# Four edits around a decomposed-bias attention: position terms in row halves, earlier q and k weights, tables on another queue, weight sums from the tenth turn

## The chip, the cores and the metric

The kernel runs on one core of a Trainium2 chip. The metric is the device time of one execution in microseconds (us). In this document PE is TensorE (the matrix engine), DVE is VectorE, ACT is ScalarE, POOL is GpSimd and SP is SyncE, which here only issues transfers. PEld is the loading of a matmul's stationary operand, which the profile lists beside PE.

## The reference, cut to what matters

Four layers run one after the other on an image of 48 x 48 positions with 768 channels. Only the first layer is touched: a transformer block with 12 heads of 64 channels, whose attention adds two learned position terms to the scores. T = 2304 is the number of positions.

```python
xn = layernorm(x)
q, k, v = split(xn @ qkv_w + qkv_b)                      # 12 heads, 2304 x 64 each
attn  = (q * scale) @ k.T                                # 2304 x 2304 per head
rel_h = einsum('bhwc,hkc->bhwk', q, Rh)                  # one number per query and key row
rel_w = einsum('bhwc,wkc->bhwk', q, Rw)                  # one number per query and key column
attn  = softmax(attn + rel_h[..., :, None] + rel_w[..., None, :])
x = x + (attn @ v) @ proj_w + proj_b
x = x + gelu(layernorm(x) @ w1 + b1) @ w2 + b2
```

Three more layers (spectral filter, scan, spectral filter) follow and are the same in both kernels.

## The kernel before, in words

**Stages.** The first layer runs as: layer norm with q, k, v and the position terms (`qkv_phase`), attention (`attention_bounded`; `attention_any` is a general version behind a run-time branch, which these inputs don't take), output projection (`proj_phase`), then the two-layer perceptron (`mlp_phase`). Products of float32 matrices with weights use a seven-product scheme for 2 x 2 blocks, so weights are first combined into seven sums.

**qkv_phase** walks three superblocks `sb` of 768 tokens. In each it makes v (line 166), then q and k for six head pairs `pr` (line 297). The combined q and k weights are written to memory in superblock 0 and read back by `load_qk` (line 247) in superblocks 1 and 2, into a ring of three weight tiles (`wqk`). The position terms of a superblock are made in 24 steps that lag behind: each step loads a table `relD` (`tables`, line 381, ring of four tiles), multiplies it with q (line 417 for rows, line 403 for columns) and `split`s the result into three bfloat16 parts on ACT and DVE (lines 373 to 376), which go to memory (`rh_d`, `rw_d`, line 392). `advance` issues the tables of up to three steps ahead. The steps of the last superblock run partly after its last q and k product, in front of the attention. `ahead(0)` loads a small one-hot matrix `oneh` and keys and values of the first head pair (`kv`, lines 527 and 528); `ahead(1)` loads the first chunk of queries and its position terms `bt` (lines 505, 506, 534).

**attention_bounded** works on transposed scores: keys on partitions, queries along the free axis. It walks 6 head pairs x 5 query chunks (`qc`, 464 queries, the last 448) x 18 key tiles `kt` of 128 keys. Three key tiles are a turn; there are 180 turns, and turn `i` issues in this order:

- `products` for three key tiles (line 576): for each of the two heads a float32 matmul with 64 contraction rows, head 0 in the upper half of the array's rows and head 1 in the lower half;
- `scores` for three key tiles: for each head one bfloat16 matmul (line 585) with 120 contraction rows (48 column parts and 72 row parts of the position terms, `bt`, against `oneh`) that adds the position terms in PSUM, then the exponential of both heads on ACT (line 587) into a tile `p`, then an addition on DVE (line 595) for the softmax denominators;
- `values` of turn `i - 1` (line 606): for each head a float32 matmul with 64 output columns, the heads in the two column halves of the array. At the end of a chunk `row_sums` (lines 614 and 616) and `finish` (line 622).

The score tiles `s` have three PSUM buffers and `p` has ten SBUF buffers. Beside this, a generator `other` prepares the weights of the projection and the perceptron (`weight_sums`): in every sixth turn it takes one step, with loads on SP (line 776), combinations on POOL (lines 131 to 134) and stores. Its input tiles (`pw0b` is the first) come out of the ring of `p`. The generator has 29 steps; the turns 3, 9, ..., 177 offer 30.

**What sets the order.** A scheduler fixes every engine's order, SP's included, when the program is built; an engine then works strictly in that order. SP's instructions of all loads and stores stand in one queue, and each waits in its place for what it needs.

Of the kernel before, what the change touches and what calls it, by code (L numbers as in the profile page):

```python
# [182 lines left out]
def qkv_phase(tc, ident, x, qkv_w, qkv_b, relT, rel_d, ln_g, ln_b, q_d, k_d, v_d, rw_d, rh_d, wqk_d, wv_d, flag, home, ahead):  # L183
# [18 lines left out]
    with (  # L202
# [42 lines left out]
        def load_qk(sb, pr):  # L245
            wqks[sb, pr] = w_tile(f"wqk_{sb}_{pr}").rearrange("p (n c f) -> p n c f", n=7, c=NC2)
            nc.sync.dma_start(wqks[sb, pr], wqk_d[pr])
# [22 lines left out]
        def q_and_k(sb, have_q, step):  # L270
# [4 lines left out]
            for pr in range(NC):  # L275
                if sb:
                    if (sb, pr) not in wqks:
                        load_qk(sb, pr)
                    w = wqks.pop((sb, pr))
                else:  # L280
                    w = w_tile(f"wqk_{sb}_{pr}").rearrange("p (n c f) -> p n c f", n=7, c=NC2)
                    wb = wp.tile([P, NC2, P], F32, tag="wb", name=f"wb_{pr}", bufs=2)
                    lo, hi = slice(pr * P, (pr + 1) * P), slice(C + pr * P, C + (pr + 1) * P)
                    nc.sync.dma_start(w[:, 0:2].rearrange("p a c f -> p (a c) f"), wv[:, :, lo])
                    nc.sync.dma_start(w[:, 6], wv[:, NC2:, hi])
                    nc.sync.dma_start(wb, wv[:, :NC2, hi])
# [40 lines left out]
                for o, d, m in ((q[:, pr], q_d, qms), (kt, k_d, kms)):  # L327
                    o = o.rearrange("p b t -> p (b t)")
                    nc.scalar.dma_start(d[pr * P : (pr + 1) * P, tok], o)
                    V.tensor_reduce(m[:, pr, sb : sb + 1], o, axis=AX.X, op=ALU.max, apply_absolute_value=True)  # L330
                if pr == 1 and sb + 1 == NSB:
                    ahead(0)
# [33 lines left out]
        with tc.tile_pool(name="qkv_o", bufs=1, side="right") as op:  # L366
            R = 2 * G

            def split(ps, parts, n):
# [6 lines left out]
                V.tensor_tensor(parts[2], r, parts[1], ALU.subtract)  # L376

            def tables(which, g, n):

                d = qp.tile([P, 4, R], F32, tag="relD", name=f"relD_{which}_{g}_{n}", bufs=4)  # L380
                nc.sync.dma_start(d, rel_d[which, g])
                return d
# [96 lines left out]
            V.tensor_reduce(mx, ps[:1, : 2 * NC], axis=AX.X, op=ALU.max)  # L479
            V.tensor_scalar(flag, mx, SAFE, None, ALU.is_lt)  # L480
            for _ in range(4):
                advance()
# [25 lines left out]


def queries(qc):  # L510

    return slice(qc * QB, min(T, (qc + 1) * QB))


def load_onehot(nc, pool, oneh_d, o):

    f = pool.tile([P, 3, P], F32, tag="onehf", name="onehf")
    nc.sync.dma_start(f[:NBR], oneh_d)
    nc.vector.tensor_copy(o[:NBR], f[:NBR])


def attention_loads(nc, q_d, k_d, v_d, rw_d, rh_d):
# [7 lines left out]
    def chunk(qb, c):  # L530
        pr, qc = c
        q = queries(qc)
        n = q.stop - q.start
        nc.sync.dma_start(qb[0][:, :n], q_d[pr * P : (pr + 1) * P, q])
        for s in range(2):
            load_bias(nc, qb[1][:, s, :, :, :n], rw_d, rh_d, 2 * pr + s, q.start, n)

# [3 lines left out]
def attention_bounded(tc, ahead, oT, beside, load_next):  # L541
# [14 lines left out]
    with (  # L556
# [22 lines left out]
        def scores(c, kt):  # L579
# [3 lines left out]
            ps = scs.pop((c, kt))  # L583
            for s in range(2):
                nc.tensor.matmul(ps[:, s, :n], lhsT=oneh[:NBR, b % 3, :], rhs=held(c)[1][:NBR, s, b // 3, j, :n], start=False, stop=True)  # L585
            p = pp.tile([P, 2, QB], F32, tag="p", name=f"p_{pr}_{qc}_{kt}")[:, :, :n]
# [39 lines left out]
        for i in range(len(work) + 1):  # L626
            if i % 6 == 3:
                next(other, None)
            if i == len(work) - 8:
                load_next()  # L630
            if i < len(work):
# [8 lines left out]
                for kt in range(k0, k0 + KB):  # L640
                    products(c, kt)
                for kt in range(k0, k0 + KB):
                    scores(c, kt)
# [11 lines left out]

def attention_any(tc, ident, oneh, q_d, k_d, v_d, rw_d, rh_d, oT, beside, load_next):

# [8 lines left out]
    with (  # L666
# [8 lines left out]
        ones = cp.tile([1, HD], F32, tag="ones", name="an_ones")  # L675
        nc.vector.memset(ones, 1.0)
        ka = cp.tile([HD, T], F32, tag="ka", name="an_ka")
        vt = cp.tile([P, NT, HD + 1], F32, tag="vt", name="an_vt")
# [632 lines left out]
def block_kernel(ctx: ExitStack, tc: tile.TileContext, a: dict):  # L1311
# [19 lines left out]
    atc = at_stack.enter_context(tc.tile_pool(name="at_c", bufs=1, side="left"))  # L1331
    oneh = atc.tile([P, 3, P], BF16, tag="oneh", name="oneh")

# [3 lines left out]
    def load_ahead(stage):  # L1337
        if stage == 0:
            load_onehot(nc, atc, a["oneh"], oneh)
# [7 lines left out]
        ones = pool.tile([P, HD], F32, tag="ones", name="ones")  # L1347
        nc.vector.memset(ones, 1.0)
        ahead.extend((loads, kvs, qbs, ones, oneh))
# [18 lines left out]
    with which.Else():  # L1368
        attention_any(tc, ident, oneh, q_d, k_d, v_d, rw_d, rh_d, oT, beside, load_pw)
    at_stack.close()  # L1370
# [486 lines left out]
```

## Time and profile before

| | us |
|---|---|
| median of three runs | 3815.2 (3811.54 to 3820.01) |
| profiled execution | 3815.61 |
| its span | 3813.4 |
| qkv and position terms | 0 to 512.6 |
| attention | 512.6 to 1671.2 |
| projection | 1671.2 to 1810 |
| perceptron and part of the next layer | 1810 to 2820 |
| spectral filter, scan, spectral filter | 2820 to 3813 |

The stages are read from the first instruction of each in the timeline. Of the attention's 1158.6 us PE is busy 1153.05, at a granted clock of 1.00. A matmul in float32 stands as two records in the profile, one in bfloat16 as one. A row of a timeline gives start, duration, engine, line, operation, output and inputs, shapes, and in brackets the idle time of the engine before it with what ended it; a row of the waits gives total, times and longest.

### The profile page before, as it was taken

Reading aid. Unit: us, or ns where it says so; the run is one execution under the profiler, and the core shown is the slowest. Engines: PE = TensorE matmul, PEld = TensorE weight load, DVE = VectorE, ACT = ScalarE, POOL = GpSimd, SP = SyncE. Lnnn points to the kernel's source line nnn. Section 1 sums busy time; section 2 is a strip of 40 time slices with the busy share of each in tenths; the row PEclk is TensorE's granted clock in tenths of the full one; section 3 lists DMA queues with packets and bytes.
Section 4 is the critical chain, followed back from the end, with each engine's and each line's share of the span. In section 5 each row is a group of like instructions: output and inputs, shape, how many; then the busy total and the mean of one; then the engine's idle time right before and its main releaser. Section 6 shows DMA issues by size and latency. Waiting matters only on the chain.

```text
span 3813.4 us, 51839 instructions
## 1 busy us (share of the span) xinstructions
PE 3707.4 (97%) x20914; PEld 2168.0 (57%) x20914; DVE 2032.0 (53%) x3070; ACT 1135.3 (30%) x1803; POOL 653.5 (17%) x498
## 2 busy tenths in 40 slices
PE   7999979999999999998999999999999998999998
PEld 4666543333333333345555555555568876996685
DVE  6655455656566666565424433232325567995455
ACT  1323244444444444420310120011013356222342
POOL 3101001111111111025000000000013301981131
PEclk9999989999999999999999999999999999999999
DMA  7655563333332322124334534443454402112345
GB/s 261 209 191 190 182 189 121 114 108 114 102 101 90 101 90 76 50 86 156 133 105 134 172 109 126 134 133 108 125 161 110 112 29 94 40 33 73 98 117 154
DMA packets 276271, 460.28 MB, mean 121 GB/s; under 512 B 50909, under 2 KB 228821, under 8 KB 269527
## 3 DMA queue, kind: packets, MB, share of 16 engines
q1 hardware_dynamic: 266215, 435.94, 37.5%
q10 hardware_dynamic: 9808, 20.94, 1.5%
q8 instruction: 167, 2.74, 0.3%
q14 instruction: 81, 0.66, 0.1%
HBM read 318.49 MB, written 138.31 MB: 120 GB/s over the span
## 4 chain that ended last, share of the span: by engine, by line
PE 87%; DVE 4%; POOL 3%; DMA 3%; ACT 1%; issue 1%; SPq 0%; ACTq 0%; POOLq 0%; DVEq 0%
PE p L886 13%; PE p L949 13%; PE s L576 12%; PE av L606 11%; PE qk L297 6%; PE s L585 6%; PE c L1113 4%; PE v L166 3%; POOL t L1214 2%; PE pj L166 2%; PE f_z L1516 2%; PE f_z L1517 2%; PE f_x L1481 2%; PE so L1291 2%; PE f_u L1531 2%; PE rh L417 1%
## 5 line engine op out<-in xcount | busy, mean ns | idle before, releaser
L595 DVE TENSOR_TENSOR acc<-acc,p 128x928 f32<-128x928 f32 (+1 forms) x480 | 561.6, 1170 | 359.4 <-ACT p L587 328.1
L587 ACT ACTIVATE p<-s 128x928 f32<-128x928 f32 (+1 forms) x540 | 467.9, 940 | 681.5 <-PE s L585 575.1
L949 PE MATMUL p<-w,h 128*128 128x384 f32 x1512 | 492.7, 486 | 0.0
L576 PE MATMUL s<-qt,kv 64*128 64x464 f32 (+1 forms) x2160 | 467.8, 565 | 7.6 <-ACT p L587 5.4
L606 PE MATMUL av<-p,kv 128*64 128x464 f32 (+1 forms) x2160 | 456.3, 557 | 0.0
L949 PEld LDWEIGHTS p<-w,h 128*128 128x128 f32 x1512 | 286.2, 190 | 196.9
L576 PEld LDWEIGHTS s<-qt,kv 64*128 64x128 f32 x2160 | 194.2, 187 | 277.5 <-issue 161.9
L886 PE MATMUL p<-x2nT,w 128*128 128x384 f32 x864 | 293.9, 490 | 3.3 <-issue 3.3
L606 PEld LDWEIGHTS av<-p,kv 128*64 128x64 f32 x2160 | 141.9, 136 | 247.1 <-issue 237.8
L297 PE MATMUL qk<-xnT,wqk 128*128 128x384 f32 x756 | 252.5, 491 | 5.0 <-DMA wqk<-wqk_d 5.0
L1206 PE MATMUL c<-H,bands 128*48 128x96 f32 x5632 | 243.8, 247 | 11.4 <-issue 10.9
L1206 PEld LDWEIGHTS c<-H,bands 128*48 128x48 f32 x5632 | 234.8, 123 | 20.6 <-issue 11.3
L585 PE MATMUL s<-bt,oneh 120*128 120x464 bf16 (+1 forms) x1080 | 241.3, 359 | 0.0
L886 PEld LDWEIGHTS p<-x2nT,w 128*128 128x128 f32 x864 | 165.4, 192 | 119.2 <-issue 6.1
L886 PE MATMUL p<-xT,w 128*128 128x384 f32 x648 | 220.8, 486 | 0.0
L297 PEld LDWEIGHTS qk<-xnT,wqk 128*128 128x128 f32 x756 | 144.6, 193 | 99.8 <-issue 8.3
L585 PEld LDWEIGHTS <-oneh 120*128 120x128 bf16 x1080 | 90.9, 98 | 190.8 <-issue 110.3
L925 POOL TENSOR_TENSOR rr<-rr,ml_b 128x1152 f32<-128x1152 f32 x12 | 31.5, 2622 | 955.6 <-DMA rr<-xr_d 863.6
L881 ACT ACTIVATE h<-h,ml_b 128x384 f32<-128x384 f32 x144 | 88.3, 614 | 346.6 <-DVE h L901 174.3
L1214 POOL TENSOR_TENSOR t<-s,c 128x768 f32<-128x768 f32 x80 | 144.5, 1832 | 179.5 <-DMA bands<-in_bands_dram 168.9
L886 PEld LDWEIGHTS p<-xT,w 128*128 128x128 f32 x648 | 123.1, 190 | 85.9
L616 DVE RECIPROCAL rec<-rs 128x464 f32<-128x464 f32 (+1 forms) x30 | 91.1, 3038 | 98.7 <-PE rs L614 98.7
(322 smaller groups left out, 4792.6 us busy)
## 6 DMA issues: line engine op xcount, KB each, us to landing
w<-w1s_d SPq DMA_DIRECT2D x36, 768.0 KB
w<-w2s_d SPq DMA_DIRECT2D x36, 768.0 KB
w<-w1s_d SPq DMA_DIRECT2D x36, 576.0 KB
w<-in_mlp_w_dram SPq DMA_DIRECT2D x27, 768.0 KB
wqk<-wqk_d SPq DMA_DIRECT2D x12, 1344.0 KB
yu<-f_ys SPq DMA_DIRECT2D x24, 672.0 KB
f_yt<-yu SPq DMA_DIRECT2D x20, 720.0 KB
yu<-f_us SPq DMA_DIRECT2D x18, 720.0 KB
```

The lines of the kernel that those rows point to most:

```text
L166: nc.tensor.matmul(p[:, :TB], lhsT=rhs[n][:, c, t * P : (t + 1) * P], rhs=w[:, c, :], start=c == 0, stop=c == NC2 - 1)
L297: nc.tensor.matmul(p[:, :TB], lhsT=w[:, n, c, :], rhs=ops[sb][n][:, c, :], start=c == 0, stop=c == NC2 - 1)
L576: nc.tensor.matmul(ps[:, s, :n], lhsT=keys[pr % 2][rows, kt * P : (kt + 1) * P], rhs=held(c)[0][rows, :n], start=True, stop=False)
L585: nc.tensor.matmul(ps[:, s, :n], lhsT=oneh[:NBR, b % 3, :], rhs=held(c)[1][:NBR, s, b // 3, j, :n], start=False, stop=True)
L587: nc.scalar.activation(p, ps[:, :, :n], AF.Exp)
L595: nc.vector.tensor_tensor(probs[c], probs[c], p, ALU.add)
L606: nc.tensor.matmul(avs[c][rows, : size(c)], lhsT=vals[pr % 2][:, kt, rows], rhs=p[:, s, :], start=kt == 0, stop=kt == NT - 1)
L886: nc.tensor.matmul(p[:, :TB], lhsT=w[n][:, c, :], rhs=rhs[n][:, c, :], start=c == 0, stop=c == NC2 - 1)
L949: nc.tensor.matmul(ps[t][:, :TB], lhsT=hs[left, f][:, t * P : (t + 1) * P], rhs=wt[:, f % KW2, :], start=f == 0, stop=f == NF2 - 1)
L1113: nc.tensor.matmul(ps[:K, i, :n], lhsT=v[:, c, tok : tok + K], rhs=w[:, cc, c0 : c0 + n], start=cc == NC - 1, stop=cc == 0)
L1206: nc.tensor.matmul(ps[r0 : r0 + G, k // 4, cols], lhsT=bands[:, n - GC, i, :] if gr else bands0[:, n, i, :], rhs=H[:, n, :, d : d + NPR], ...
L1214: GP.tensor_tensor(t, sc[:, ch], c1[:, m0 : m0 + GC].unsqueeze(2).to_broadcast([P, GC, RR, NPR]), ALU.mult)
```

## The change

- **Position terms in row halves.** The 120 contraction rows of a head's position terms are cut into 64 (48 column parts and 16 row parts) and 56 (the other row parts). Head 0 has its rows in partitions 0 to 63, head 1 in 64 to 127, so that all of these matmuls have the same row halves as `products`. Each head and key tile now has two bfloat16 matmuls in place of one. The order within a turn becomes products and scores of the first key tile, then of the second, then of the third. `bt` and `oneh` have new layouts, with new loads (`load_bias_halves`: ten transfers for a stretch of tokens in place of eight; `load_onehot_halves`: four and four copies in place of one and one).
- **q and k weights** are requested two pairs ahead in superblocks 1 and 2, and `ahead(0)` is called after pair 4 of the last superblock in place of pair 1.
- **Last tables on another queue.** After the bound for the branch is computed, `tables` issues on ACT's queue in place of SP's.
- **Weight sums from the tenth turn.** Turn 3 is skipped: the 29 steps use the turns 9 to 177.
- `ones` is set at the start of the program, in another pool. `attention_any` loads its own `oneh`.

```diff
@@ q_and_k
-                    if (sb, pr) not in wqks:
-                        load_qk(sb, pr)
+                    if pr + 2 < NC:
+                        load_qk(sb, pr + 2)
...
-                if pr == 1 and sb + 1 == NSB:
+                if pr == 4 and sb + 1 == NSB:
                     ahead(0)
@@ qkv_phase
+            queue = [nc.sync]
+
             def tables(which, g, n):
                 d = qp.tile([P, 4, R], F32, tag="relD", name=f"relD_{which}_{g}_{n}", bufs=4)
-                nc.sync.dma_start(d, rel_d[which, g])
+                queue[0].dma_start(d, rel_d[which, g])
...
             V.tensor_scalar(flag, mx, SAFE, None, ALU.is_lt)
+            queue[0] = nc.scalar
             for _ in range(4):
                 advance()
@@ new functions
+def load_bias_halves(nc, bt, rw_d, rh_d, c, t0, n):
+    nw = 3 * KTW
+    at = t0
+    while at < t0 + n:
+        sb, t = divmod(at, 2 * TB)
+        m = min(2 * TB - t, t0 + n - at)
+        cols = slice(2 * c * TB + t, 2 * c * TB + t + m)
+        dst = bt[:, :, at - t0 : at - t0 + m]
+        for s in range(2):
+            w = rw_d[s].rearrange("(j k) n b f -> j (k n) b f", j=KJ)[:, :, sb, cols].rearrange("j r t -> r j t")
+            r = rh_d[s].rearrange("(a k) n b f -> a (k n) b f", a=2)[:, :, sb, cols]
+            p0 = s * HD
+            for a in range(2):
+                nc.sync.dma_start(dst[p0 : p0 + nw, a * KJ : (a + 1) * KJ], w)
+                nc.sync.dma_start(dst[p0 + nw : p0 + HD, a * KJ : (a + 1) * KJ], r[a, : HD - nw].unsqueeze(1).to_broadcast([HD - nw, KJ, m]))
+            nc.sync.dma_start(dst[p0 : p0 + NBR - HD, 2 * KJ :], r[:, HD - nw :].rearrange("a r t -> r a t"))
+        at += m
...
+def load_onehot_halves(nc, pool, oneh_d, o):
+    f = pool.tile([P, 2, 3, P], F32, tag="onehf", name="onehf")
+    for s in range(2):
+        p0 = s * HD
+        nc.sync.dma_start(f[p0 : p0 + HD, 0], oneh_d[:HD])
+        nc.sync.dma_start(f[p0 : p0 + NBR - HD, 1], oneh_d[HD:])
+        nc.vector.tensor_copy(o[p0 : p0 + HD, 0], f[p0 : p0 + HD, 0])
+        nc.vector.tensor_copy(o[p0 : p0 + NBR - HD, 1], f[p0 : p0 + NBR - HD, 1])
@@ attention_bounded: scores
-            for s in range(2):
-                nc.tensor.matmul(ps[:, s, :n], lhsT=oneh[:NBR, b % 3, :], rhs=held(c)[1][:NBR, s, b // 3, j, :n], start=False, stop=True)
+            for k in range(2):
+                for s in range(2):
+                    rows = slice(s * HD, s * HD + (NBR - HD if k else HD))
+                    rhs = held(c)[1][rows, 2 * KJ + b // 3 if k else b // 3 * KJ + j, :n]
+                    nc.tensor.matmul(ps[:, s, :n], lhsT=oneh[rows, k, b % 3, :], rhs=rhs, start=False, stop=k == 1)
@@ attention_bounded: the turns
-            if i % 6 == 3:
+            if i % 6 == 3 and i > 3:
                 next(other, None)
...
                 for kt in range(k0, k0 + KB):
                     products(c, kt)
-                for kt in range(k0, k0 + KB):
                     scores(c, kt)
@@ block_kernel
-    oneh = atc.tile([P, 3, P], BF16, tag="oneh", name="oneh")
+    oneh = atc.tile([P, 2, 3, P], BF16, tag="oneh", name="oneh")
+    ones = atc.tile([P, HD], F32, tag="ones", name="ones")
+    nc.vector.memset(ones, 1.0)
...
-        qbs = [(pool.tile([P, QB], F32, tag=f"qt{i}", name=f"qt{i}"), pool.tile([P, 2, 2, KJ, QB], BF16, tag=f"bt{i}", name=f"bt{i}")) for i in range(2)]
+        qbs = [(pool.tile([P, QB], F32, tag=f"qt{i}", name=f"qt{i}"), pool.tile([P, 2 * KJ + 2, QB], BF16, tag=f"bt{i}", name=f"bt{i}")) for i in range(2)]
```

More of the change, by code (lines that the diff above doesn't have):

```diff
@@ L534, in chunk @@
         nc.sync.dma_start(qb[0][:, :n], q_d[pr * P : (pr + 1) * P, q])
-        for s in range(2):
-            load_bias(nc, qb[1][:, s, :, :, :n], rw_d, rh_d, 2 * pr + s, q.start, n)
+        load_bias_halves(nc, qb[1][:, :, :n], rw_d, rh_d, pr, q.start, n)
     return keys_values, chunk
@@ L583, in scores @@
             ps = scs.pop((c, kt))
-            for s in range(2):
-                nc.tensor.matmul(ps[:, s, :n], lhsT=oneh[:NBR, b % 3, :], rhs=held(c)[1][:NBR, s, b // 3, j, :n], start=False, stop=True)
+            for k in range(2):
[3 more added lines that the diff above has]
+                    nc.tensor.matmul(ps[:, s, :n], lhsT=oneh[rows, k, b % 3, :], rhs=rhs, start=False, stop=k == 1)
             p = pp.tile([P, 2, QB], F32, tag="p", name=f"p_{pr}_{qc}_{kt}")[:, :, :n]
@@ L653, in attention_bounded, with attention_any @@
             pass
-def attention_any(tc, ident, oneh, q_d, k_d, v_d, rw_d, rh_d, oT, beside, load_next):
+def attention_any(tc, ident, oneh_d, q_d, k_d, v_d, rw_d, rh_d, oT, beside, load_next):
     nc = tc.nc
@@ L676, in attention_any @@
         nc.vector.memset(ones, 1.0)
+        oneh = cp.tile([P, 3, P], BF16, tag="oneh", name="an_oneh")
+        load_onehot(nc, cp, oneh_d, oneh)
         ka = cp.tile([HD, T], F32, tag="ka", name="an_ka")
@@ L1338, in load_ahead @@
         if stage == 0:
-            load_onehot(nc, atc, a["oneh"], oneh)
+            load_onehot_halves(nc, atc, a["oneh"], oneh)
             kv_tile()
@@ L1344, in load_ahead @@
         pool = at_stack.enter_context(tc.tile_pool(name="at_a", bufs=1, side="left"))
-        qbs = [(pool.tile([P, QB], F32, tag=f"qt{i}", name=f"qt{i}"), pool.tile([P, 2, 2, KJ, QB], BF16, tag=f"bt{i}", name=f"bt{i}")) for i in range(2)]
+        qbs = [(pool.tile([P, QB], F32, tag=f"qt{i}", name=f"qt{i}"), pool.tile([P, 2 * KJ + 2, QB], BF16, tag=f"bt{i}", name=f"bt{i}")) for i in range(2)]
         loads[1](qbs[0], (0, 0))
-        ones = pool.tile([P, HD], F32, tag="ones", name="ones")
-        nc.vector.memset(ones, 1.0)
         ahead.extend((loads, kvs, qbs, ones, oneh))
@@ L1368, in block_kernel @@
     with which.Else():
-        attention_any(tc, ident, oneh, q_d, k_d, v_d, rw_d, rh_d, oT, beside, load_pw)
+        attention_any(tc, ident, a["oneh"], q_d, k_d, v_d, rw_d, rh_d, oT, beside, load_pw)
     at_stack.close()
```

## The prediction

> **What bounds the kernel now.** I read the page first, then the attention's stage, then one turn of it, then the places where PE stands still. PE carries the page, and the attention's three matmuls (lines 576, 585, 606) are a third of its work:
>
> ```profile
> PE 3707.4 (97%) x20914; PEld 2168.0 (57%) x20914; DVE 2032.0 (53%) x3070; ACT 1135.3 (30%) x1803; POOL 653.5 (17%) x498
> ...
> L576 PE MATMUL s<-qt,kv 64*128 64x464 f32 (+1 forms) x2160 | 467.8, 565 | 7.6 <-ACT p L587 5.4
> L606 PE MATMUL av<-p,kv 128*64 128x464 f32 (+1 forms) x2160 | 456.3, 557 | 0.0
> ...
> L585 PE MATMUL s<-bt,oneh 120*128 120x464 bf16 (+1 forms) x1080 | 241.3, 359 | 0.0
> ```
>
> Line 576 idles 7.6 us in 2160 matmuls, the other two never: from 512.6 to 1671.2 only PE's own pace counts. What that pace is made of shows in one turn's weight loads (start, duration), since a pass starts with its load:
>
> ```profile
> 1022.93 0.30 PEld L576 LDWEIGHTS s<-qt,kv 64*128 64x128 f32 x4 [0.73 <-issue]
> 1023.43 0.19 PEld L576 LDWEIGHTS s<-qt,kv 64*128 64x128 f32 x2 [0.20 <-issue]
> ...
> 1024.60 0.19 PEld L576 LDWEIGHTS s<-qt,kv 64*128 64x128 f32 x2 [0.20 <-issue]
> 1025.47 0.90 PEld L585 LDWEIGHTS <-oneh 120*128 120x128 bf16 x6 [0.68 <-issue]
> 1026.75 0.20 PEld L606 LDWEIGHTS av<-p,kv 128*64 128x64 f32 x4 [0.38 <-DVE acc L595]
> 1027.19 0.14 PEld L606 LDWEIGHTS av<-p,kv 128*64 128x64 f32 x2 [0.24 <-issue]
> ...
> 1028.36 0.14 PEld L606 LDWEIGHTS av<-p,kv 128*64 128x64 f32 x2 [0.25 <-issue]
> 1029.23 0.30 PEld L576 LDWEIGHTS s<-qt,kv 64*128 64x128 f32 x4 [0.73 <-ACT p L587]
> ```
>
> A turn lasts 1029.23 - 1022.93 = 6.30. Both heads' passes run together and follow each other at 0.389 in float32 (1023.43 to 1024.60 are three); the bfloat16 ones, one head after the other, at 0.196 (single records). Six of 576, six of 606 and six of 585 make 5.84. The other 0.45 lies at the three changes of shape. Into 576: the last pass of 606 starts at 1028.75 and ends its 0.389 at 1029.14, 0.10 before the next; then the first pass takes 0.50 in place of 0.39, since its load isn't hidden: 0.20 together. Into 585: 1024.60 + 2 x 0.389 = 1025.38, 0.095 early, and 0.01 for the load: 0.105. Into 606: 0.09 and 0.05, 0.14.
>
> PE's other idle time near the change is at the attention's start:
>
> ```profile
> ACT p L587 <- POOL pw0p L133: 9.6, 1, 9.6
> PE rw L403 <- DMA relD_w<-in_relD_dram: 9.3, 4, 5.8
> ```
>
> ```profile
> 504.94 5.48 PE L403 MATMUL rw<-q,relD_w 128*96 128x96 f32 x40 [5.78 <-DMA relD_w<-in_relD_dram]
> 512.66 2.61 PE L576 MATMUL s<-qt,kv 64*128 64x464 f32 x12 [2.24 <-DVE rest_w L374]
> ...
> 518.29 2.72 PE L576 MATMUL s<-qt,kv 64*128 64x464 f32 x12 [1.74 <-ACT p L587]
> ```
>
> ```profile
> 550.67 0.99 POOL L131 TENSOR_TENSOR pw0p<-pw0b,pw0p 128x384 f32<-128x384 f32 x1 [168.65 <-DMA bt<-rw_d]
> ...
> 552.64 2.62 ACT L587 ACTIVATE p<-s 128x928 f32<-128x928 f32 x3 [9.57 <-POOL pw0p L133]
> ...
> 553.64 4.11 PE L576 MATMUL s<-qt,kv 64*128 64x464 f32 x12 [3.65 <-ACT p L587]
> ```
>
> Tables keep PE waiting 9.3 us in four pieces before 512.66. The exponential of the sixth turn waits until POOL gives back `pw0b`, a tile of the ring of `p`; its load was issued at 544.88, behind a saturated queue.
>
> **The change part by part.** In the built order of both kernels PE's sequence outside the attention is the same, so the sum is made in these places.
>
> Row halves. Matmuls of 585 double, but the two heads run side by side, so a key tile still costs two passes of 0.196: 64 rows of both heads, then 56 of both. That they run together is read from 576: two heads' records start 7 ns apart there and share a pass of 0.389. A turn then needs six passes of each as before. What goes is the change into full rows: 576 and 585 have one shape now. 180 turns x 0.105 = 18.9 us. The change into 606 stays. Loads: each bfloat16 load is 0.098 in the records, under a pass of 0.196; the float32 load behind a bfloat16 pass keeps PE 0.105 when it isn't hidden, and 0.105 fits in 0.196.
>
> Here a rule speaks against the change. The row: in line 576 loads of the same row halves start with each pass, and the passes stay 0.389 apart, so nothing of the load shows. The Trainium skill, page "TensorE: Matmul & The Clock Gate", "What overlaps and what doesn't" in its Part 3, says that weight loads overlap matmuls in flight only in another row group. By that rule each of the 1080 bfloat16 double passes would show its load: 0.01 (585's first) to 0.105 (576's first) each, 11 to 113 us. By the row it is 0, which I take, as it is the same rows and the same neighbours.
>
> New order of a turn. The first exponential may start after 1.3 us of a turn in place of 2.9. In the steady state it waits for nothing, gain 0. In the first turn ACT loads its table (1.28 us) behind the first score, so the second turn's 1.74 falls: first score done at 1.45, table to 2.9, exponential to 3.9, PE's first turn 3.5: 0.4 left, gain 1.4. At a chunk's end DVE gets an addition ahead of the reciprocal (3.06): denominators at 4.7 into the turn, then 3.06 + 1.17 + 0.63 gives 9.6, while the next 606 starts at 10.7. Covered by 1.1; without cover 30 chunk ends would cost it.
>
> Weight sums from turn 9. The stall of 3.65 goes, and with it the stretched line 576 behind it (4.11 for 2.54): 5.2 us. What is late next: `pw0b`'s load stands behind the `bt` load that waits for turn 8, like `pw1b` before, which POOL had finished at about 579 with its use at about 590. For the double tiles of the last twelve steps the exponential that waits moves earlier in its chunk (key tile 14 in place of 15). Loads at 1186.5 gave a first store at 1192.1 and a second at 1195.1, landing (estimate, 2.5 more) by 1195 and 1198; the exponentials come 12.6 and 16.5 after the load. Covered by at least 3.
>
> Last tables on ACT's queue. SP drops 14 loads, so that none stands behind the `bt` loads and the `rh_d` store (that is the 5.78). But ACT now casts and issues: 32 casts at some 0.45 in sequence and eight tables at 0.35 (its own stores are 0.33) are 17 us. It may begin when the first column product is done (about 489.4; in the new order ACT takes two of those casts before the row casts), so the last cast comes at 507 to 509 in place of 512.95, and PE's start follows at about 509 instead of 512.66. Gain 3.5; bounds: 9.3, all waits gone, and -3, if the tables land as late as now (4.8 us from issue for two of them) and hold up the casts.
>
> q and k weights, and `ahead`. The wait is 5.0 us for pair 1 at 397.26. SP around it:
>
> ```profile
> 372.50 0.59 SPq L528 DMA_DIRECT2D kv<-v_d  x1
> 373.18 3.04 SPq L392 DMA_DIRECT2D rw_d<-rw  x2
> 376.61 3.71 SPq L236 DMA_DIRECT2D v_d<-v_o  x1
> 380.37 3.73 SPq L247 DMA_DIRECT2D wqk<-wqk_d  x1
> ```
>
> In the new build's order these four stand unchanged; the values of `kv` are still first, although their call moved. Only pairs 2 and 3 pass the keys' load, where nothing waited. Gain 0; up to 5.0 if the queue drains faster. Superblock 1 keeps its order.
>
> Rest. `oneh`: three more loads and three copies of some 0.4 in superblock 0, where PE has no idle time: 0, without cover 1.2. `bt`: ten transfers for eight, 0.4 each on SP, which is free for most of a chunk of 38 us; its partition rows fall from 720 to 496 per head: 0.
>
> Sum: 18.9 + 1.4 + 5.2 + 3.5 = 29.0. The profiled execution took 3815.6, the median of runs 3815.2: 3786.2.
>
> **The rivals.**
>
> Slower: PE drains when the data type changes, not only at a change of tiling. Into 585 both change, so the row can't tell. The new turn has three changes to bfloat16 (0.105 each) and two back (0.20, with an exposed load): 5.84 + 0.20 + 0.315 + 0.40 + 0.14 = 6.90, 0.60 more than now, 108 us less 10 from the start: 3913. It decides from 0.16 us per turn, 32 ns per change of type. Against it: 606 to 576 has one type and loses the same 0.10, so shape alone explains it; and the skill's "TensorEngine Tiling (Array Packing)", Key Properties, names only the tiling mode. By it 18.9 gained, by the rival 108 lost.
>
> The drain stays: passes in halves cost a few ns more each (9 ns on twelve would do), and only the start gains: 3815.2 - 10.1 = 3805.
>
> The start gives nothing: ACT as the table's issuer is as late as SP, and the tile of `p` stalls once elsewhere. 3815.2 - 18.9 - 1.4 = 3795.
>
> **How the numbers follow.** Forecast 0.60 (own range 3778 to 3793), drain stays 0.15, start gives nothing 0.09, drain per type 0.12, more than forecast (pair 1's wait goes too, tables in full: 3775) 0.04. The range 3773 to 3807 leaves out the slow case. About 0.2% (7.6 us) is what a measurement of this kernel can tell from no change. The forecast, 3795 and 3775 and half of the 3805 case are faster: 0.81; the other half of it is nearly all of same, 0.07; slower 0.12.
>
> **What would show it.** A turn of 6.19 with weight loads of 576 and 585 in turn and no gap of 0.1 between them; a turn near 6.9 or passes of 585 further apart than 0.2 prove me wrong. Line 576's idle near 0.4 besides the first start, no exponential waiting for POOL; the attention's first matmul near 509; the 5.0 at line 297 still there.

## The result and the profile after

| | before | after |
|---|---|---|
| median | 3816.15 (3811.54 to 3820.01) | 3788.78 (3788.09 to 3789.85) |
| profiled execution, its span | 3815.61, 3813.4 | 3788.09, 3786.2 |
| attention's first matmul | 512.66 | 511.15 |
| projection's first matmul | 1672.02 | 1646.44 |

The times are in microseconds. The ratio of the medians is 0.9928, with a 95% interval of 0.9913 to 0.9943. By the profiles the changed kernel leads by 1.5 us when the attention begins, by 25.6 when it ends (at the projection's first matmul) and by 27.4 at the last matmul. So the attention itself gave 24.1.

The page after, the lines that answer to those shown of before (line 576 is now 610, 585 is 622, 606 is 643):

```profile
PE 3689.9 (97%) x21994; PEld 2185.2 (58%) x21994; DVE 2049.4 (54%) x3073; ACT 1174.9 (31%) x1803; POOL 668.4 (18%) x498
...
L610 PE MATMUL s<-qt,kv 64*128 64x464 f32 (+1 forms) x2160 | 527.5, 564 | 2.3 <-DVE rest_w L374 2.3
...
L643 PE MATMUL av<-p,kv 128*64 128x464 f32 (+1 forms) x2160 | 455.6, 557 | 0.0
...
L622 PE MATMUL s<-bt,oneh 64*128 64x464 bf16 (+3 forms) x2160 | 301.4, 355 | 0.0
```

The count of position matmuls doubled. Line 610's idle time is 2.3 us, all of it ahead of the first matmul of the attention; the 5.4 that it spent on exponentials is gone. Busy time by line misleads here: 610 went from 467.8 to 527.5 and 622 from 241.3 to 301.4, although a turn got shorter. The ends of matmuls overlap their successors, and where two lines take turns each is charged with its own tail. The timeline of PE gives the turn (start, duration):

```profile
1020.57 1.05 PE L610 MATMUL s<-qt,kv 64*128 64x464 f32 x4
1021.46 0.56 PE L622 MATMUL s<-bt,oneh 64*128 64x464 bf16 x4
1021.85 0.95 PE L610 MATMUL s<-qt,kv 64*128 64x464 f32 x4
1022.63 0.56 PE L622 MATMUL s<-bt,oneh 64*128 64x464 bf16 x4
1023.03 0.94 PE L610 MATMUL s<-qt,kv 64*128 64x464 f32 x4
1023.81 0.56 PE L622 MATMUL s<-bt,oneh 64*128 64x464 bf16 x4
1024.29 2.56 PE L643 MATMUL av<-p,kv 128*64 128x464 f32 x12
1026.78 1.05 PE L610 MATMUL s<-qt,kv 64*128 64x464 f32 x4
```

Two of PEld's rows in the same turn:

```profile
1021.65 0.39 PEld L610 LDWEIGHTS s<-qt,kv 64*128 64x128 f32 x4
1022.25 0.10 PEld L622 LDWEIGHTS <-oneh 64*128 64x128 bf16 x2 [0.20 <-issue]
```

A turn is 1026.78 - 1020.57 = 6.21, where it was 6.30. Read the distances of starts: two float32 passes 1021.85 to 1022.63 are 0.78, which is 2 x 0.389; two bfloat16 passes 1021.46 to 1021.85 are 0.39, which is 2 x 0.196. Neither change of type leaves a gap: the weights of the product at 1021.85 are loaded from 1021.65 on, in the same rows, while the last bfloat16 pass runs. Over all turns of 464 queries the median went from 6.303 to 6.207, of 448 queries from 6.103 to 6.007.

The waits of PE from 300 to 560 us and the start of the attention:

```profile
PE rw L405 <- DMA relD_w<-in_relD_dram: 5.6, 5, 4.3
PE qk L297 <- DMA wqk<-wqk_d: 4.7, 1, 4.7
PE bound L479 <- DVE pz L475: 3.3, 1, 3.3
PE s L610 <- DVE rest_w L374: 2.3, 1, 2.3
```

```profile
502.76 1.56 PE L405 MATMUL rw<-q,relD_w 128*96 128x96 f32 x8 [4.26 <-DMA relD_w<-in_relD_dram]
...
511.15 1.05 PE L610 MATMUL s<-qt,kv 64*128 64x464 f32 x4 [2.32 <-DVE rest_w L374]
512.00 0.82 PE L622 MATMUL s<-bt,oneh 64*128 64x464 bf16 x4
512.55 1.82 PE L610 MATMUL s<-qt,kv 64*128 64x464 f32 x4
...
522.56 1.05 PE L610 MATMUL s<-qt,kv 64*128 64x464 f32 x4
```

PE still waits for the tables, 5.6 us in place of 9.3. The first turns run slow: a group of four matmuls of line 610 takes 1.82, and 0.95 later. The first two turns take 522.56 - 511.15 = 11.41, where before they took 524.71 - 512.66 = 12.05.

### The profile page after: what moved, and what is told of

Same layout as the page of the kernel before. It is cut to its first block, busy times and chain, and to the rows that moved or that the text cites. A ratio compares the mean times of both kernels' runs of the same rounds, so it can differ in the third digit from the quotient of the medians.

```text
span 3786.2 us, 54130 instructions
## 1 busy us (share of the span) xinstructions
PE 3689.9 (97%) x21994; PEld 2185.2 (58%) x21994; DVE 2049.4 (54%) x3073; ACT 1174.9 (31%) x1803; POOL 668.4 (18%) x498
## 2 busy tenths in 40 slices
DMA packets 259478, 448.23 MB, mean 118 GB/s; under 512 B 47426, under 2 KB 212018, under 8 KB 252724
## 5 line engine op out<-in xcount | busy, mean ns | idle before, releaser
L632 DVE TENSOR_TENSOR acc<-acc,p 128x928 f32<-128x928 f32 (+1 forms) x480 | 574.2, 1196 | 308.9 <-ACT p L624 274.1
L624 ACT ACTIVATE p<-s 128x928 f32<-128x928 f32 (+1 forms) x540 | 507.1, 939 | 620.0 <-PE s L622 616.4
L610 PE MATMUL s<-qt,kv 64*128 64x464 f32 (+1 forms) x2160 | 527.5, 564 | 2.3 <-DVE rest_w L374 2.3
L622 PE MATMUL s<-bt,oneh 64*128 64x464 bf16 (+3 forms) x2160 | 301.4, 355 | 0.0
L622 PEld LDWEIGHTS <-oneh 64*128 64x128 bf16 (+1 forms) x2160 | 108.4, 93 | 259.9 <-issue 255.7
L1244 PE MATMUL c<-H,bands 128*48 128x96 f32 x5632 | 244.2, 247 | 12.2 <-issue 10.9
L1244 PEld LDWEIGHTS c<-H,bands 128*48 128x48 f32 x5632 | 234.5, 123 | 22.1 <-issue 11.3
L1554 PE MATMUL f_z<-f_w,f_o 97*96 97x96 f32 x800 | 133.6, 249 | 0.0
```

What stands on the lines that cost most here:

```text
L610: nc.tensor.matmul(ps[:, s, :n], lhsT=keys[pr % 2][rows, kt * P : (kt + 1) * P], rhs=held(c)[0][rows, :n], start=True, stop=False)
L622: nc.tensor.matmul(ps[:, s, :n], lhsT=oneh[rows, k, b % 3, :], rhs=rhs, start=False, stop=k == 1)
L624: nc.scalar.activation(p, ps[:, :, :n], AF.Exp)
L632: nc.vector.tensor_tensor(probs[c], probs[c], p, ALU.add)
L1244: nc.tensor.matmul(ps[r0 : r0 + G, k // 4, cols], lhsT=bands[:, n - GC, i, :] if gr else bands0[:, n, i, :], rhs=H[:, n, :, d : d + NPR], ...
L1554: nc.tensor.matmul(out, lhsT=o1[:, j, 1:3, :].rearrange("c r h -> c (r h)"), rhs=w2t[:, b, 0, :], start=True, stop=False)
```

## The experiments

Each ratio is against the kernel before on the same chip, whose median there lies between 3817.0 and 3820.03. The first row and those with "alone" are edits of the kernel before, the others of the changed kernel.

| kernel | median | ratio, interval |
|---|---|---|
| full rows, alternating order | 3921.13 | 1.0270 (1.0256 to 1.0284) |
| row halves, grouped order | 3796.93 | 0.9946 (0.9932 to 0.9960) |
| weight sums from the tenth turn alone | 3812.9 | 0.9988 (0.9981 to 0.9994) |
| last tables on ACT's queue alone | 3816.03 | 0.9999 (0.9991 to 1.0008) |
| row halves and alternating order alone | 3796.97 | 0.9950 (0.9936 to 0.9963) |
| q and k two pairs ahead alone | 3819.56 | 1.0003 (0.9995 to 1.0011) |
| changed, tables on SP's queue again | 3790.78 | 0.9926 (0.9912 to 0.9939) |
| changed, SP's queue, five tables ahead | 3786.52 | 0.9919 (0.9906 to 0.9933) |
| changed, pair 1's weights on ACT's queue | 3780.35 | 0.9904 (0.9889 to 0.9919) |
| the last two together | 3775.34 | 0.9890 (0.9873 to 0.9906) |
| that, with the tables on ACT's queue | 3779.77 | 0.9898 (0.9881 to 0.9914) |

### Is it the shape or the data type, the halves or the order?

Two kernels, each with one of the two parts of the edit (row halves, new order). The kernel before with products and position terms in turn, full rows:

```diff
                 for kt in range(k0, k0 + KB):
                     products(c, kt)
-                for kt in range(k0, k0 + KB):
                     scores(c, kt)
```

> The kernel before with one edit: products and scores of a key tile follow each other, with the position terms still in 120 full rows. A turn then has six changes of tiling in place of three. Theory A (each change of shape drains PE for 0.10 us and shows the next load: 0.105 into the position terms, 0.20 back into the products): a turn is 6.303 + 2 x 0.105 + 2 x 0.20 = 6.91 us, the kernel about 110 us slower than before, near 3925. Theory D (the 0.10 belongs to the end of a long group of matmuls and not to the change of shape): the turn stays near 6.3 and the time near 3815.

Its PE timeline, one turn:

```profile
1026.24 1.05 PE L576 MATMUL s<-qt,kv 64*128 64x464 f32 x4
1027.22 0.56 PE L585 MATMUL s<-bt,oneh 120*128 120x464 bf16 x2
1027.72 1.05 PE L576 MATMUL s<-qt,kv 64*128 64x464 f32 x4
...
1033.16 1.05 PE L576 MATMUL s<-qt,kv 64*128 64x464 f32 x4
```

The turn is 6.92. A key tile takes 1027.72 - 1026.24 = 1.48, where the halves take 1.18 (1023.03 - 1021.85). The price of a change of shape, read before from a single place, holds at three: 5.84 + 3 x (0.20 + 0.105) + 0.14 = 6.90. Four position matmuls in halves cost PE the same 0.39 as two in full rows, so nothing but the changes differs.

The changed kernel in grouped order, so that the type changes once each way in a turn where it changed three times:

```diff
                 for kt in range(k0, k0 + KB):
                     products(c, kt)
+                for kt in range(k0, k0 + KB):
                     scores(c, kt)
```

> The changed kernel with the old order inside a turn: the products of three key tiles, then the scores of three. Theory A (the gain is the row halves: products and scores have one shape, the order does not matter): a turn stays at 6.20 to 6.21 us in place of 6.303 before and 6.207 after, and the time stays within 3 us of the changed kernel; only the second turn waits longer for the first exponential again (about 1 us). Theory B (the alternation is what saves): a turn goes back to about 6.30, 17 us slower than the changed kernel. Theory C (a change of data type costs something small, and alternating pays it five times more per turn): a turn is shorter than 6.207, down to 6.19.

```profile
1022.81 2.61 PE L610 MATMUL s<-qt,kv 64*128 64x464 f32 x12
1025.25 1.35 PE L622 MATMUL s<-bt,oneh 64*128 64x464 bf16 x12
1026.53 2.56 PE L643 MATMUL av<-p,kv 128*64 128x464 f32 x12
1029.02 2.61 PE L610 MATMUL s<-qt,kv 64*128 64x464 f32 x12
```

The turn is 6.21 again (median 6.209 against 6.207). Two more changes of type each way cost nothing that shows; the drain is that of the shape. The order is worth something at the two ends: in this profile the first two turns take 13.41 instead of 11.41, and from the last turn's first product to the projection 10.85 pass instead of 9.74, so that the lead at the attention's end is 3.5 us smaller than the changed kernel's. The time missed the 3 us of the expectation: the lead over the kernel before is 20.1 us by the medians, 7.3 less than the changed kernel's. In the profiles the other 3.6 us arise behind the attention, where the code is the same, and stay unexplained.

### The weight sums

```diff
-            if i % 6 == 3:
+            if i % 6 == 3 and i > 3:
                 next(other, None)
```

> The kernel before with the weight sums from turn 9 alone. Theory A: the exponential of the sixth turn no longer waits for POOL; 5.2 us less (ratio 0.9986), all of it in turns 5 and 6 (10.02 and 8.59 us become 6.30 and 7.08), every other turn as before. Rival: the tile pw0b is late one chunk later, and the same wait shows in turn 11 or 12; then 0 to 2 us less.

PE's timeline around the place of the stall, where line 576 stood at 553.64 behind 3.65 of idle time:

```profile
551.38 2.61 PE L576 MATMUL s<-qt,kv 64*128 64x464 f32 x12
...
558.46 2.61 PE L576 MATMUL s<-qt,kv 64*128 64x464 f32 x12
```

There is no idle time here, and the turn at a chunk's end takes 558.46 - 551.38 = 7.08, as later ones do. Its attention began 1.5 us later than before's and its first row sums came 3.8 earlier: 5.2 us gained. By the medians 4.1 us of it are seen (the kernel before had 3817.0 on this chip).

The row halves and the new order with the three other edits undone show what the stall does beside them. The edits, made to the changed kernel:

```diff
-                    if pr + 2 < NC:
-                        load_qk(sb, pr + 2)
+                    if (sb, pr) not in wqks:
+                        load_qk(sb, pr)
...
-                if pr == 4 and sb + 1 == NSB:
+                if pr == 1 and sb + 1 == NSB:
...
-            queue[0] = nc.scalar
...
-            if i % 6 == 3 and i > 3:
+            if i % 6 == 3:
```

> The changed kernel with three of its edits undone: weight sums again from the fourth turn, the last tables again on SP's queue, q and k weights and ahead(0) as before. What is left is the row halves and the alternating order. Theory A (the turn's 0.096 us is the drain at the change of shape, and edits add up): 180 turns x 0.096 = 17.3 us, about 0.5 us in the first two turns, about 1.1 us at the attention's end, no gain before the attention: turns of 6.21, the stall of about 5 us near the sixth turn is back, attention start within 1 us of 512.7, and the total about 18 to 19 us under the kernel before, ratio 0.9951. Rival (the edits lean on each other; part of the 17.3 or of the end's 1.1 needs the stall removed): total within 15 us of the kernel before, ratio 0.996 or more.

PE's timeline, then ACT's, then POOL's (the products stand in line 609 here):

```profile
539.85 1.05 PE L609 MATMUL s<-qt,kv 64*128 64x464 f32 x4
...
554.42 1.92 PE L609 MATMUL s<-qt,kv 64*128 64x464 f32 x4 [8.29 <-ACT p L623]
```

```profile
553.42 2.62 ACT L623 ACTIVATE p<-s 128x928 f32<-128x928 f32 x3 [15.01 <-POOL pw0p L133]
```

```profile
551.45 0.99 POOL L131 TENSOR_TENSOR pw0p<-pw0b,pw0p 128x384 f32<-128x384 f32 x1 [168.94 <-DMA bt<-rw_d]
```

The stall is now 8.29, and the two turns take 14.57 and 9.90 where 6.21 and 6.99 are usual: 11.3 us lost, in place of 5.2. The sum says why. PE reaches this place at 554.42 - 8.29 = 546.13, where before it came at 549.99, 3.86 earlier; POOL's combinations begin at 551.45 in place of 550.67, 0.78 later. The two make 4.64, and the idle time grew by 8.29 - 3.65 = 4.64. The load of `pw0b` was issued at 544.88 before and at 545.15 here, so PE's lead brought it no earlier: what PE gained ahead of the load is given back there to the last tenth. Skipping turn 3 is worth 5.2 us alone and 11 beside the row halves. The rest of the 11.3 is the clock, which is lowered behind the stall (a window; span, busy time and instructions of PE, PEld, DVE, ACT and POOL, then the granted clock, the DMA engines' busy share and GB/s):

```profile
550.15:560.30 10.15, 5.88 (x20) 2.59 (x22) 3.98 (x3) 4.39 (x5) 4.86 (x4) 0.50 0.28 100
```

PE works at half its clock from 554.42 to 560.3 and loses half of these 5.9 us: 8.29 + 2.95 = 11.2. In the kernel before the clock was 0.50 from 553.3 to 556.7, so 3.65 + 1.5 = 5.2.

At the projection the lead is 15.7 us, which the parts make up: 1.6 at the attention's start, where none was expected, 17.3 for the shape, 1.7 in the first two turns, 1.1 at the end, less 6.0 for the longer stall. The total is 20.6 us under the kernel before, near Theory A's 18 to 19, but with the start and the stall mis-sized, and with 3.3 us of lead that appeared behind the attention.

### The last tables

```diff
+            queue = [nc.sync]
+
             def tables(which, g, n):
...
-                nc.sync.dma_start(d, rel_d[which, g])
+                queue[0].dma_start(d, rel_d[which, g])
...
+            queue[0] = nc.scalar
             for _ in range(4):
                 advance()
```

> The kernel before with the last tables on ACT's queue alone. My sum said 3.5 us; the changed kernel's trace shows its attention starting 1.5 us earlier, with three tables held 4.3 us behind a store of row terms and loads of position terms. Theory A (the transfers' common bandwidth, not the issuing queue, sets when these tables land): 1 to 2 us less, PE waits for tables 5 to 7 us before the attention in place of 9.3. Rival (in the old layout the position terms are more bytes in the same stretch, so the tables land later still): 0 to 1 us less.

PE's waits from 300 to 560 in this kernel:

```profile
PE rw L405 <- DMA relD_w<-in_relD_dram: 5.4, 5, 1.9
```

The wait for tables fell from 9.3 to 5.4 and the attention started at 512.72, where it was 512.66. The bound's matmul had come 0.9 later, so that the stretch from it to the attention is 0.9 shorter; of the 3.9 that the wait lost, other links of the chain took 3.0. The first two turns were slower (13.61), the stall of the weight sums was shorter in this profile, and so nothing of it is left in the time. By the medians the kernel is 1.0 us under the one before, inside the noise (0.9991 to 1.0008). The opposite test is the changed kernel without this edit:

```diff
-            queue[0] = nc.scalar
```

> The changed kernel with one edit undone: the last tables again on SP's queue. Theory A (the ACT queue brings nothing, and its four scattered waits let the granted clock fall just as the attention begins): the tables' wait is again one of about 5.4 us plus smaller ones, the attention's first matmul comes within 1 us of 511.15, but at the full clock, so that the first two turns take about 10.2 us in place of 11.41; total within 2 us of the changed kernel, rather below it. Rival (the 1.5 us by which the changed kernel's attention starts earlier came from the queue): first matmul at 512.7 or later, first two turns about 11.4, total 1 to 3 us above the changed kernel.

Its PE timeline:

```profile
505.03 6.07 PE L405 MATMUL rw<-q,relD_w 128*96 128x96 f32 x40 [5.01 <-DMA relD_w<-in_relD_dram]
512.79 1.05 PE L609 MATMUL s<-qt,kv 64*128 64x464 f32 x4 [1.69 <-DVE rest_w L374]
```

Its start, 512.79, is the rival's number and outside the 1 us that I gave; its first two turns, 10.17, are Theory A's. Its median is 2.0 above the changed kernel's, measured on another chip, and the two ratios agree (0.9926 and 0.9928), so the time doesn't tell the two apart. The start has to be counted from the bound's matmul, since this profile reached that one 2.5 us later than the changed kernel's for another reason (6.2 us at line 297). From the bound's second record to the attention's first matmul the profiles give (tables read five ahead left out):

| position terms | tables on SP | tables on ACT |
|---|---|---|
| full rows | 29.82, 29.87, 29.92, 30.01 | 29.01 |
| row halves | 27.83, 27.86 | 28.61, 28.65, 28.67 |

So the queue alone brings 0.9, and loses 0.8 once the position terms are in halves. The halves bring 2.0 with the tables on SP: the last five tables, issued from 499.40 on before and from 501.83 on here, let PE go on 5.5 and 3.2 us later. `bt` in halves has fewer bytes (the whole kernel moves 448.23 MB in place of 460.28), and stands just ahead of these tables on the queue; that the bytes are the reason was not tested by itself.

The clock in the same stretch, first of the changed kernel, then of the one with SP's queue (columns as above):

```profile
510.00:515.00 5.00, 3.85 (x18) 2.29 (x20) 1.92 (x4) 2.98 (x4) 0.00 (x0) 0.72 0.41 84
```

```profile
510.00:515.00 5.00, 3.31 (x25) 2.21 (x26) 3.31 (x7) 2.80 (x7) 0.00 (x0) 0.97 0.01 3
```

With the tables on ACT the attention begins at a clock of 0.72, and its first two turns cost 1.24 more. All five profiles with ACT's queue begin so; of the eight on SP's queue two are slow in these turns as well. What decides can be read from the clock's course. In these traces it is 1.00 or 0.50 and changes on a grid of 3.41 us. The changed kernel's last two steps of this grid around the attention's start, then the step that holds the start in the kernel with SP's queue:

```profile
508.80:512.20 3.40, 1.08 (x8) 0.59 (x9) 3.01 (x6) 1.91 (x4) 0.00 (x0) 1.00 0.00 0
512.20:515.60 3.40, 3.40 (x14) 1.97 (x12) 0.00 (x0) 2.65 (x3) 0.00 (x0) 0.50 0.77 159
```

```profile
510.40:513.70 3.30, 1.61 (x15) 1.05 (x15) 2.83 (x6) 2.19 (x5) 0.00 (x0) 1.00 0.00 0
```

PE is busy for 0.32 of the first and for 0.49 of the last, and only the first is followed by half the clock. In all five profiles with ACT's queue the step ahead of the fall was busy for 0.23 to 0.32; in the six others that begin at full clock the step around or just ahead of the start was busy for 0.43 to 0.64. Where the grid lies against the attention's start differs from profile to profile, so how much of this is the queue and how much chance is not shown.

### The q and k weights

> The kernel before with the q and k weights loaded two pairs ahead and ahead(0) after pair 4, nothing else. Theory A (the load of pair 1's weights still stands behind the values, the rw_d store and the v_d store on SP): the wait at line 297 stays between 4.5 and 5.2 us, the attention starts within 0.5 us of 512.66, the total is unchanged, ratio 1.000. Rival (the call's new place frees the queue and the row halves only hid it): the wait at line 297 falls below 2 us and the attention starts 3 to 5 us earlier, ratio 0.999.

The edit is the first two hunks of the change, alone. PE's waits:

```profile
PE qk L297 <- DMA wqk<-wqk_d: 5.3, 1, 5.3
```

Nothing moved in the wait or in the time (1.0003, 0.9995 to 1.0011). The attention began at 511.53, 1.1 us earlier and so outside the 0.5 of the expectation, but the bound's matmul was 1.2 earlier already. The next run goes at the wait itself, in the changed kernel:

```diff
-            nc.sync.dma_start(wqks[sb, pr], wqk_d[pr])
+            (nc.scalar if (sb, pr) == (NSB - 1, 1) else nc.sync).dma_start(wqks[sb, pr], wqk_d[pr])
```

> The changed kernel with one transfer moved: the q and k weights of pair 1 in the last superblock are loaded over ACT's queue instead of SP's. Theory A (PE waits 4.7 us at line 297 because that load stands behind three transfers on SP): the wait falls under 1 us, the attention starts 3 to 4.5 us earlier than 511.15, the total is about 3785, ratio to the kernel before 0.9918. Rival (the transfers share the same saturated DMA engines, or the next pair's weights are late in its place): the wait stays over 3 us or turns up at pair 2, start within 1 us of 511.15, total unchanged against the changed kernel.

The wait is gone, and the attention begins at 503.36, 7.8 us earlier than the changed kernel's, where 3 to 4.5 were expected and only 4.7 were waited. The windows (columns as above) of the changed kernel, then of this one:

```profile
395.00:400.00 5.00, 2.90 (x5) 1.72 (x6) 0.00 (x0) 0.00 (x0) 0.00 (x0) 0.62 1.02 416
400.00:405.00 5.00, 5.00 (x12) 2.69 (x12) 0.56 (x1) 0.65 (x2) 0.00 (x0) 0.70 0.91 360
```

```profile
395.00:400.00 5.00, 5.00 (x17) 2.95 (x16) 1.11 (x2) 0.61 (x1) 0.00 (x0) 1.00 0.98 352
400.00:405.00 5.00, 5.00 (x17) 2.94 (x16) 2.67 (x5) 0.72 (x2) 0.00 (x0) 1.00 0.81 337
```

PE is busy for all of 400 to 405 in both and gets 12 matmuls done in one, 17 in the other. The granted clock of the changed kernel is 0.62 in the window in which the wait ends and 0.70 in the next. The lowered clock has a sharp edge:

```profile
396.20:403.00 6.80, 5.90 (x10) 3.21 (x11) 0.00 (x0) 0.48 (x1) 0.00 (x0) 0.50 0.99 407
```

PE works again from 397.10, so 5.9 us at half the clock lose 2.95: with the wait 7.65 of the 7.8. The DMA engines are as full in both (0.55 to 1.2 in each 5 us from 370 to 395), and the earlier issue from another queue was enough to have the load in time.

### Towards a better version

The tables on SP again, with more of them read ahead:

```diff
-                d = qp.tile([P, 4, R], F32, tag="relD", name=f"relD_{which}_{g}_{n}", bufs=4)
+                d = qp.tile([P, 4, R], F32, tag="relD", name=f"relD_{which}_{g}_{n}", bufs=6)
...
-                while len(ready) < 3 and steps:
+                while len(ready) < depth[0] and steps:
...
+                if sb + 1 == NSB:
+                    depth[0] = 5
...
-            queue[0] = nc.scalar
```

> The changed kernel with the last tables again on SP's queue, but a ring of 6 tables in place of 4 and five tables read ahead in place of three in the last superblock. Theory A (what PE waits for at the attention's start is the issue and landing of the last tables, so earlier issue helps): the waits for tables there fall from about 5.6 us in the changed kernel to under 3, and the attention's first matmul comes at 509 to 510.5 in place of 511.15; total 1 to 2 us under the changed kernel. Rival (the casts on ACT and DVE set the pace, or the last three tables, which still stand behind the next queries' position terms on SP, come as late as before): first matmul at 511 to 513, total within 1.5 us of the changed kernel or slower.

```profile
503.33 4.12 PE L405 MATMUL rw<-q,relD_w 128*96 128x96 f32 x24 [7.13 <-DMA relD_w<-in_relD_dram]
508.70 1.92 PE L611 MATMUL s<-qt,kv 64*128 64x464 f32 x4 [1.25 <-DVE rest_w L374]
```

The attention starts at 508.70, earlier than the 509 to 510.5 of Theory A, and not for its reason: from bound to start it takes 28.58, as good as the changed kernel's 28.67, and the waits became one of 7.13. The gain was there at 245 us (line 297 goes on at 241.33 in place of 244.76): between 150 and 300 us PE waits 1.8 us for the copies of `xnT`, where it waited 4.0. The transposes that stood at 195 us in the changed kernel come later, so the larger ring had changed the built order there.

Both edits together, and then with the tables on ACT's queue:

> The changed kernel with pair 1's q and k weights of the last superblock on ACT's queue, and the last tables on SP's queue with a ring of 6 and five read ahead. Theory A (the two gains are in different places and add): no wait at line 297, 7 to 8 us from it and from the lowered clock behind it; 2 to 3 us from the deeper ring, which lie before 230 us; attention's first matmul at about 501, total about 3778, ratio 0.9896. Rival (the deeper ring's 3 us were an accident of its order and do not come again): first matmul at 503 to 504, total about 3780.5, ratio 0.9904.

> As the other kernel of this call, but the last tables on ACT's queue as in the changed kernel. Theory A (the one wait of 7.1 us that the deeper ring left was that of the last three tables behind the next queries' position terms on SP): that wait falls under 3 us, the attention's first matmul comes at 496 to 499, total 3 to 5 us under the kernel with SP, about 3774, ratio 0.9886. Rival (the casts on ACT, or the DMA engines that all queues share, set the time of the last table): tables' wait still over 4 us, total within 1.5 us of the kernel with SP.

With SP's queue the attention begins at 500.17, and the two gains add: 3775.34 is 42 us under the kernel before on the same chip and 13 under the changed kernel's median, the fastest of all. With ACT's queue the waits of PE become these:

```profile
PE s L612 <- DVE rest_w L374: 4.6, 1, 4.6
PE rw L405 <- DVE rest_w L374: 3.3, 5, 2.5
...
PE rw L405 <- DMA relD_w<-in_relD_dram: 0.9, 1, 0.9
```

Here the tables are no longer late (0.9), and the attention still begins only 27.65 us after the bound. The casts that split the results on ACT and DVE take the place: Theory A was right on the wait and wrong on the start. The first two turns cost 1.5 more than with SP, at the lowered clock again. The total is 4.4 above the kernel with SP, where 3 to 5 below were expected; 0.8 of it are there at the attention's end, the rest arises behind it and is not explained.

## Why the prediction was right, and where its steps were not

Forecast 29.0 us and 3786.2; measured 27.4, median 3788.78. The largest step came out for the reason given; two of the smaller ones did not. Step by step:

- **Row halves: right.** 0.096 of a turn in place of 0.105, so 180 x 0.096 = 17.3 for 18.9. The rule of the Trainium skill that was set against it (page "TensorE: Matmul & The Clock Gate", "What overlaps and what doesn't" in Part 3: weight loads overlap matmuls in flight only in another row group) would have made each double pass show its load, 11 to 113 us. The measurement decides against reading it so: passes stay 0.389 and 0.196 apart with a load for every matmul in the same row halves. The rivals "drain per data type" and "drain stays" are both out: the type costs nothing (6.209 against 6.207), and with halves 0.009 of the 0.105 is left in a turn.
- **New order in the first turns: the step was right, its cover was not looked at.** 1.4 was forecast. With the clock full it is 12.05 - 10.17 less two turns' 0.19, 1.7. In the changed kernel it is 0.64 - 0.19 = 0.45, since the attention began at a granted clock of 0.72. The sum took a full clock for granted, although in before's profile it is 0.50 from 502.1 to 508.9, at the same waits.
- **Weight sums: right.** Forecast 5.2. The turns of 10.02 and 8.59 around the stall became 6.21 and 6.99, 5.4 with 0.19 of it the shape: 5.2. No exponential waits for POOL anywhere in the attention. The sum did not see that the other edits would have doubled this stall if it had stayed.
- **Last tables on ACT's queue: wrong by its size, and by its sign.** 3.5 was forecast, 1.5 came, and not from there. The step that failed is "PE's start follows at about 509": a wait was counted as time to gain, where a chain of casts ends hardly sooner. The last cast, forecast for 507 to 509, ends at 511.54, where it ended at 512.95. By the table above this edit brings 0.9 alone, and costs 0.8 beside the halves, and in these profiles 1.24 more in the first turns. The 1.5 at the attention's start are 2.0 of the halves, less 0.8 of the queue, and 0.3 that were there at the bound.
- **`bt` at 0: mis-sized.** The row halves brought 2.0 at the attention's start when the tables stay on SP. The prediction named the smaller rows and put them at nothing, without looking at the tables that stand behind them on the queue.
- **q and k weights and `ahead`: right, 0.** The wait at line 297 went from 5.0 to 4.7; by itself the edit leaves 5.3.
- **Not in the sum.** About 1.1 at the attention's end and 1.9 behind it. The first belongs to the new order: from the last turn's first product to the projection 9.4 to 9.9 us pass in the eight profiles with it, 10.9 to 11.1 in the five with the old one. That the last exponentials start earlier is the likely reason. The 1.9 are no finding: in the twelve kernels besides before, with the same code behind the attention, the lead changes there by -2.4 to +3.3.

The measured steps 17.3 + 0.45 + 5.2 + 1.5 + 1.1 + 1.9 make 27.4. That the total came within 3 us is in part luck: the halves, the first turns and the tables were 4.5 us too high together, and 3.0 us that were not counted, of which 1.9 are scatter, made up for most of it.

## What to carry to other kernels

When neighbouring matmuls have different tilings, look whether one tiling serves both. It paid here although it doubled the count of one group, since two heads share a pass and the number of passes stayed the same; each change of shape that goes is worth its gap and its exposed load. Price a wait of PE by what lies behind it too: add half of the time for which the lowered clock outlasts it, and look for the next late transfer, which takes back all that was gained ahead of it. Before taking a load's wait away, ask which chain on other engines ends at nearly the same time.

## What the runs showed of the hardware

- A change between float32 and bfloat16 in one tiling costs PE nothing that shows in a turn (6.209 and 6.207 us with one and three changes each way); a change into full rows and back costs 0.30 (a key tile of 1.48 in place of 1.18).
- A bfloat16 position matmul in half the rows runs beside the other head's: four of them take the 0.39 us of two in full rows.
- A single wait of 4.7 us of PE cost 7.8: the clock was 0.50 from 396.2 to 403.0, and PE's work was back at 397.10. The waits of 3.65 and 8.29 at the weight sums cost 5.2 and 11.3 by the same sum.
- In the thirteen traces, from 30 us on, all 108 of the 3.41 us steps at full clock in which PE's records cover less than 0.40 of the time are followed by half the clock; of 143 with 0.40 to 0.70 it is 42, of 13774 with more none. The clock comes back only behind a step with 0.81 or more. The page named above ("HAM oscillation — how this bites in real kernels") warns of gaps of more than about 3.4 us. The wait of 4.7 us agrees; but the 2.3 us ahead of the attention, in a step busy for 0.32, was followed by half the clock as well.
- Two weight loads for the same product, one queue apart: in SP's queue the load was issued at 380.27 and PE waited 4.7 us for it; in ACT's it was issued at 373.22 and in time, with the DMA engines as full.
